# Attention and a routed FFN on one core: another order of the last block's stages, of the softmax sums' way through DRAM and of the first gathers of the second table

## The chip, the core and the metric

The kernel runs on one core of a Trainium2 chip. The metric is the time on the device in microseconds (us), lower is better. A profiled execution gives times of single instructions by the engines: TensorE (PE, matmuls; PEld, its weight loads), VectorE (DVE), ScalarE (ACT), GpSimd (POOL) and SyncE (SP, which here only issues DMAs).

## The reference, cut to what matters

All data is float32: x of 4 batches, 1024 tokens and 256 channels.

```python
x = x + attention(_layernorm(x), w_attn, w_proj)   # causal, 16 heads of 16, ALiBi bias
x = x + ffn(_layernorm(x))
# ffn attends, at each of the 1024 positions, over the 4 batches:
qkv = x @ in_proj_w.T + in_proj_b
scores = einsum('tbhd,sbhd->bhts', q, k) * scale   # t, s: the 4 batches; b: 1024 positions
ctx = softmax(scores) applied to v
h = _layernorm(x + ctx @ out_w.T + out_b, ln1_g, ln1_b)
logits = h @ router_w.T + router_b
assign = max of the two best experts' numbers      # 8 experts, so 1 to 7
out = w2[assign] @ gelu(w1[assign] @ h + b1) + b2  # only the assigned expert counts
result = _layernorm(h + out, ln2_g, ln2_b)
```

A token has exactly one expert, so the kernel computes one expert for a token, in tiles of 128 tokens of the same expert.

## The kernel before, in words

**Attention** is cut into 20 units. Chunks c = 0 to 2 of 256 query columns give four units each (one a batch: u0 to u11, two blocks of 128 queries), chunk 3 gives eight units of one block (u12 to u19). A unit has four groups of heads (G = 4), and each group its rounds: scores by PE (`score`, L884), exp by ACT (L892), the causal zeros by POOL (L902), and two rounds later the weighted values by PE (`weigh`, pv, L925), whose extra column gives the sums of the exps. The order of PE's work is written by hand: a loop over pairs p of rounds, with an "E slot" (steps that are mostly DVE's) at 2p and 2p + 1 and a "D slot" (PE steps) between. Steps are put at numbered slots by `at_E` and `at_D`.

The **sums' way** of a unit: after its last pv, `weigh` writes y to DRAM (SP, L941). `load_sums` reads the sums back, one to a partition (L948); `invert` takes reciprocals on DVE (L955) and writes them, r, to DRAM (L956); `load_y` reads r spread over each head's channels, su (L971), and y, yc (L974); `divide` multiplies them on DVE (L979); `project` does the output projection on PE (op, L991) and adds to x on DVE (L984). With e the first pair behind the unit, these stand at E slots 2e + 3, 2e + 5, 2e + 6, 2e + 9 and at D slot e + 5 (one earlier each, from `invert` on, for u18).

A **front** (`front(i)`, L1421) takes block i of 128 positions with its 4 batches up to the router, as a generator of stages: norm (L725, L731, L747), transposes (utp, L1448), qkvp (L1469), pr and sc (scores over batches on DVE, L1490 and L1491), softmax (tot is its sum), pv (L1510), ctp (L1533), ao (L1556) with its add (L1561), the second norm (rstd_h), key, best, rank, expert and hot (L1576 to L1605: the router's choice as 0 or 1), rows written to DRAM (L1609), place (L1614: a token's rank within its expert, by a matmul with a triangle). Fronts 0 to 6 are queued behind their chunk's last unit and yield ("E" or "D", cost); `take_E` and `take_D` run at most so much cost in a slot (2.5 or 3.6, and 5.6). Front 7 goes last, behind attention.

**Routing** (class `Routing`): `tabulate_first` runs behind six fronts and gives the full tiles among them (18), `tabulate_rest` behind all eight, 20 more. `counts` sums `so_far` over partitions by a matmul with ones (L1106), compares with the multiples of 128 (L1115) and reduces (L1120), which is the tiles of each expert. `own_of` (L1125) marks a column's expert, `looked_up` (L1137, L1140) finds the place of its first tile, in_tile (L1229, L1234, L1237) marks the tile of each token, `spread` makes at_places (L1099, its rank within the tile), and `who` (L1266) multiplies them on PE: the row of each place of a tile. From it come rows_ (gather), out_rows (scatter) and at_w (the expert's weight address).

**Tiles** (class `Experts`): `fetch` issues the gather of a tile by POOL (indirect DMA into one of 18 buffers given, L1647) and its w1 by SP (L1663, 8 buffers); a tile reaches mtp (transpose, L1674) at the third step behind its gather, then hid (L1687), gelu (ACT, L1696), oe (L1703; three PSUM buffers of a pair of tiles). Each pair is finished by stats_v (DVE), rstd_v (POOL pow, L731), o (DVE, L1720 and L1723) and two outs (POOL memset and indirect DMA, L1729 and L1730), spread over the next steps.

**The tail's order**: after attention come the tail's pools, normalise of the last groups, the last unit's sums and w2 (L1997), eight `fetch`es, `project_slots` (L1028: op of u19, with no way through DRAM), and then a loop: in each pair of slots four `tile_step`s between E and D slots. While a front is not done, `tile_step` returns at once when only HELD_BACK = 6 tiles are left or when the tile work costed for PE is ahead of that for DVE. `tabulate_rest` is put at the head of the running stages by front 7's last one. Here is the step of the loop:

```python
def tile_step():
    if queue or running and part.placed < NT:
        if experts.left() <= HELD_BACK or busy["PE"] > busy["DVE"]:
            return
```

Of the kernel before, what the change touches and what calls it, by code (L numbers as in the profile page):

```python
# [37 lines left out]
P = 128  # L38
# [29 lines left out]
HELD_BACK = 6  # L68
TILE_PE, TILE_DVE = 2.6, 1.6
# [503 lines left out]
def fast_layer(ctx: ExitStack, tc: tile.TileContext, odd, x, wq, wk, wv, wp, w_in, w_out, w_r,  # L573
# [146 lines left out]
    def norm_stats(src, n, name, tag=""):  # L720
        stats = small.tile([P, B, 6], F32, tag="stats" + tag, name=f"stats_{name}")
        mv = small.tile([P, B, 2], F32, tag="mv" + tag, name=f"mv_{name}")
        rstd = small.tile([P, B], F32, tag="rstd" + tag, name=f"rstd_{name}")
        for i in range(n):
            nc.vector.bn_stats(stats[:, i], src(i))  # L725
            nc.vector.bn_aggr(mv[:, i], stats[:, i])
        nc.vector.tensor_scalar(rstd[:, :n], mv[:, :n, 1], EPS, None, ALU.add)
        return mv, rstd

# [334 lines left out]
    class Routing:  # L1064
# [6 lines left out]
        def prepare(self):  # L1071
# [4 lines left out]
            self.firsts = numbered("firsts", [P, N_COLUMNS], [[P, N_COLUMNS]])  # L1076
# [7 lines left out]
            )  # L1084

# [18 lines left out]
        def counts(self, n):  # L1104
            pm = bank(f"counts{n}")
            nc.tensor.matmul(pm[:, :E], ones_bf, self.so_far, start=True, stop=True)  # L1106
            count = keep.tile([P, E], F32, tag="count", name=f"count{n}")
            if n == 0:

                nc.vector.tensor_scalar(count, pm[:, :E], float(P - 1), None, ALU.subtract)  # L1110
            else:
                nc.vector.tensor_copy(count, pm[:, :E])
            some = N_COLUMNS if n else len(FIRST) * B
            full = keep.tile([P, E, N_COLUMNS], F32, tag="full", name=f"full{n}")[:, :, :some]
            nc.vector.tensor_tensor(  # L1115
                full, count.unsqueeze(2).to_broadcast([P, E, some]),
                self.firsts[:, :some].unsqueeze(1).to_broadcast([P, E, some]), ALU.is_gt,
            )
            tiles = const(f"tiles{n}", [P, E])
            nc.vector.tensor_reduce(tiles, full, AX.X, ALU.add)  # L1120
            return tiles

        def own_of(self, lo, hi):
            own = keep.tile([P, N_COLUMNS, E], F32, tag="own", name=f"own{lo}")[:, lo:hi]
            nc.vector.tensor_tensor(  # L1125
                own, con(IOTA, E).unsqueeze(1).to_broadcast([P, hi - lo, E]),
                self.expert.rearrange("p k t -> p (k t)")[:, lo:hi].unsqueeze(2).to_broadcast(
                    [P, hi - lo, E]
                ), ALU.is_equal,
            )  # L1130
            return own
# [22 lines left out]
        def tabulate_first(self):  # L1154
# [3 lines left out]
            self.tiles = self.counts(0)  # L1158
# [8 lines left out]
            own = self.own_of(0, n)  # L1167
# [9 lines left out]
            yield from self.tabulate(0, 0, N_FIRST, nowhere, self.past(0, N_TILES, self.until, "whose0"))  # L1177

        def tabulate_rest(self):

            yield "D", 0.3
            lo, hi = len(FIRST) * B, N_COLUMNS
            self.split(lo, hi)
            tiles = self.counts(1)
# [6 lines left out]
            nc.vector.tensor_tensor(before, until, tiles, ALU.subtract)  # L1191
            found = const("found", [P, N_COLUMNS])
            self.looked_up(found, self.own_of(0, N_COLUMNS), before, "behind_of")
            nc.vector.tensor_tensor(found, found, self.by_128, ALU.add)

            mine, tile_of = found[:, :lo], self.tile_of[:, :lo]
            nc.vector.tensor_tensor(mine, mine, tile_of, ALU.subtract)
            nc.vector.tensor_tensor(mine, mine, self.late[:, :lo], ALU.mult)
            nc.vector.tensor_tensor(mine, mine, tile_of, ALU.add)
# [14 lines left out]
        def tabulate(self, n, first, end, tile_of, whose):  # L1214
# [11 lines left out]
            if n == 0:  # L1226
# [7 lines left out]
            nc.vector.tensor_scalar(  # L1234
                in_tile[:, :, 1], in_tile[:, :, 2], row_no, None, ALU.mult
            )
# [4 lines left out]
            who = table("who_f", [P, 3, n_tiles])  # L1241
            if n == 0:
                nc.vector.memset(who, 0.0)
# [17 lines left out]
            else:  # L1261
                at_place = late["at_place"]
                self.spread(at_place[-1], len(FIRST) * B, N_COLUMNS)
# [6 lines left out]
                self.whose = whose()  # L1270
                nc.vector.tensor_copy(who, pm)
# [10 lines left out]
            block, at_t = (table(name, [P, n_tiles], I32) for name in ("block", "at_t"))  # L1282
            nc.vector.tensor_scalar(  # L1283
                who[:, 2], who[:, 2], -float(NOWHERE), float(NOWHERE), ALU.mult, ALU.add
            )
            nc.vector.tensor_tensor(who[:, 1], who[:, 1], who[:, 2], ALU.add)
# [4 lines left out]
                who[:, 1], block, float(P), who[:, 1], ALU.mult, ALU.add  # L1291
            )
            nc.vector.scalar_tensor_tensor(
                out_rows, at_t, float(T), who[:, 1], ALU.mult, ALU.add
# [126 lines left out]
    def front(i, fact, more, last):  # L1421
# [6 lines left out]
        yield "E", 0  # L1428
# [71 lines left out]
        yield "E", 0  # L1500
# [46 lines left out]
        if not last:  # L1547
            if i < PC * (NC - 2):
                yield "E", 0
            yield "D", 2.4  # L1550
            ct = flipped(ctx_, "ct")
        yield "D", 1.8
        for t in range(B):
# [7 lines left out]
            nc.vector.tensor_tensor(u_[:, t], u_[:, t], pm, ALU.add)  # L1561
            if t == 1:
                yield "d", 1.8
        yield "E", 2.6

        taken = small.tile([P, B, E], F32, tag="taken", name=f"taken_{i}", bufs=2)
        nc.vector.tensor_copy(taken, u_[:, :, C:])
        mv, rstd = norm_stats(lambda t: u[:, t], B, f"h_{i}")
        yield "E", 0
# [36 lines left out]
        yield "E", 2.2  # L1606
        nc.vector.tensor_tensor(u, u, wide(row(G1)), ALU.mult)
# [3 lines left out]

        pm = bank(f"place_{i}")
# [12 lines left out]
        nc.vector.tensor_reduce(part.rank[:, i], rank, AX.X, ALU.add)  # L1625
        here = small.tile([P, E], F32, tag="here", name=f"here_{i}")
        nc.vector.tensor_reduce(here, hot.rearrange("p t e -> p e t"), AX.X, ALU.add)
        nc.vector.tensor_tensor(part.so_far, part.so_far, here, ALU.add)
        part.placed += 1
        if part.placed == len(FIRST):  # L1630
            running.insert(0, Running(part.tabulate_first()))
        if part.placed == NT:
            running.insert(0, Running(part.tabulate_rest()))
# [106 lines left out]
    class Experts:  # L1740
# [21 lines left out]
        def left(self):  # L1762
            return (len(tiles_to_do) + len(self.fetched)
                    + len(self.under_way) + len(self.done) + len(self.finishing))

        def advance(self):
# [5 lines left out]
            if len(self.done) == 2 or self.done and not self.under_way:  # L1772
                late["n_oe"] += late["n_oe"] % 2
                self.finishing.append((len(self.done), finish_tiles(self.done)))
                next(self.finishing[-1][1])
                self.done = []
# [16 lines left out]
    class Running:  # L1793
        def __init__(self, stages):
            self.stages, self.slot, self.was = stages, -9, None
            self.next()
# [20 lines left out]
    def take_E(cost=0.0, most=E_SLOT):  # L1817


        slot[0] += 1  # L1820
        start_fronts()
        for it in list(running):
            if it.kind in ("E", "P") and it.slot < slot[0] - (it.kind == "P"):
                if cost and cost + it.cost > most:
                    continue
# [3 lines left out]
                if it.kind == "end":  # L1829
                    running.remove(it)  # L1830
        return cost

    def take_D(cost):

        slot[0] += 1
        for it in list(running):
            while it.kind[0] in "Dd":
                if it.kind == "DQ" and ("qkv",) in held:
                    break
                if it.kind != "d" or it.slot < slot[0]:  # L1840
                    if it.slot >= slot[0] - (it.was == "E"):
                        break
                if cost and cost + it.cost > D_SLOT:
# [24 lines left out]
    for u, (n, i, size) in enumerate(units):  # L1868
# [15 lines left out]
        if u < last_unit:  # L1884
            late_ = u == last_unit - 1
            at_E(2 * e + 3, lambda u=u: load_sums(u))
            at_E(2 * e + 5 - late_, lambda u=u: invert(u))
            at_E(2 * e + 6 - late_, lambda u=u: load_y(u))
            at_E(2 * e + 9 - late_, lambda u=u: divide(u))
            at_D(e + 5 - late_, 0.9 * size, lambda u=u: project(u))  # L1890
        if b == B - 1 and u < last_unit:
            at_E(2 * e + 11, lambda c=c, i=i, size=size: queue.extend(
# [52 lines left out]
    def D_slot(p):  # L1945
# [3 lines left out]
        return take_D(sum(cost for cost, _ in todo))  # L1949
# [21 lines left out]
    for p in range(len(rounds) // 2):  # L1971
# [10 lines left out]
        E_slot(2 * p + 1, most)  # L1982
# [4 lines left out]

    tail = ctx.enter_context(pool("tail", 1))
# [4 lines left out]
    for g in range(2, G):  # L1993
        normalise(g)
    load_sums(last_unit)
# [13 lines left out]
    project_slots()  # L2009
    p = len(rounds) // 2  # L2010
    E_slot(2 * p)
    D_slot(p)
    E_slot(2 * p + 1)
    queue.append(front(NT - 1, fact, 1, True))
# [14 lines left out]
    busy = {"PE": 0.0, "DVE": 0.0}  # L2029

    def tile_step():


        if queue or running and part.placed < NT:
            if experts.left() <= HELD_BACK or busy["PE"] > busy["DVE"]:
                return
            busy["PE"] += TILE_PE
            busy["DVE"] += TILE_DVE
        experts.fetch()
        experts.advance()  # L2040

# [4 lines left out]
    for k in range(len(FIRST) // 2):  # L2046
        at_E(2 * p + 6 + 4 * k, lambda k=k: part.spread(
            late["at_place"][k], 2 * B * k, 2 * B * (k + 1)
        ))
    at_E(2 * p + 24, check_sums)  # L2050
    fetching.clear()
    while queue or running or experts.left() or of_E or of_D:
        p += 1
        start_fronts()
# [101 lines left out]
```

## Time and profile before

| | us |
|---|---|
| median of 3 runs (lowest to highest) | 875.63 (867.71 to 877.36) |
| the profiled execution | 877.08 |
| its span, first to last instruction | 875.3 |
| PE, PEld busy | 767.9 (88%), 576.8 (66%) |
| DVE, ACT, POOL busy | 535.7 (61%), 393.1 (45%), 253.1 (29%) |
| end of the last pv (attention) | 656.70 |
| start of utp, of qkvp in front 7 | 687.17, 696.12 |
| front 7's pv on DVE begins / ao begins on PE | 744.75 / 755.37 |
| front 7's hot is made (DVE) | 768.15 |
| first gather of the second table | 789.89 |
| last out issued / end | 867.18 / 875.3 |

How to read it: times count from the span's first instruction. A row of the timeline has the start, the duration, engine, line, operation, result <- operands by the program's names and, in brackets, the idle time ahead of it and what ended it. In a table of stages each engine has its busy time and, in parentheses, its instructions; PEclk is the granted clock of TensorE as a share of the full one, then the mean share of the 16 DMA engines and GB/s. The mean granted clock of the span is 0.931. A row of waits has what waited, for what, and microseconds in total, times, and the longest.

### The profile page before, as it was taken

How to read it: one execution, taken by the hardware profiler on the slowest of the kernel's cores; microseconds unless marked ns; L12 is line 12 of the kernel's file. 1: busy time of each engine (PE TensorE's matmuls, PEld its weight loads, DVE VectorE, ACT ScalarE, POOL GpSimd, SP SyncE). 2: the span in 40 equal slices, each digit the busy share in tenths (PEclk: the TensorE clock that was granted, in tenths of full speed). 3: DMA queues.
4: the chain of work that ended last, by engine and by line, in shares of the span. 5: the costliest groups of instructions: out<-in, count | busy, mean ns of one | idle time of the engine just before them, and what ended most of it. 6: DMA issues, size and time to landing. Idle time of an engine off the chain costs nothing.

```text
span 875.3 us, 22574 instructions
## 1 busy us (share of the span) xinstructions
PE 767.9 (88%) x8981; PEld 576.8 (66%) x8981; DVE 535.7 (61%) x1275; ACT 393.1 (45%) x548; POOL 253.1 (29%) x359
## 2 busy tenths in 40 slices
PE   3998889998999999999999989989995997654993
PEld 2776667666666676666777767677773785543882
DVE  7334346339467773866687483793797668682454
ACT  1453436556555755655654554565461223100220
POOL 5432114212111211112121211121122448115685
PEclk9897979999999999999999999999996999865997
DMA  6445454524423333332554343244215563017550
GB/s 203 116 106 162 113 155 129 156 74 154 134 76 107 94 100 124 98 110 79 153 146 142 112 138 120 75 117 140 74 40 161 161 191 119 8 43 240 170 156 30
DMA packets 79108, 105.60 MB, mean 121 GB/s; under 512 B 19928, under 2 KB 59155, under 8 KB 78484
## 3 DMA queue, kind: packets, MB, share of 16 engines
q1 hardware_dynamic: 73548, 89.22, 34.7%
q0 software_dynamic: 4864, 14.16, 5.2%
q8 instruction: 73, 1.20, 0.6%
q10 hardware_dynamic: 584, 0.70, 0.3%
q14 instruction: 39, 0.32, 0.1%
HBM read 67.58 MB, written 35.12 MB: 117 GB/s over the span
## 4 chain that ended last, share of the span: by engine, by line
PE 58%; DVE 16%; issue 10%; DMA 6%; POOL 6%; ACT 2%; SPq 2%; POOLq 0%; DVEq 0%; ACTq 0%
PE sk L884 16%; PE pv L925 10%; PE qkvp L1469 8%; PE qkp L803 5%; PE op L991 3%; PE vp L824 3%; PE ao L1556 2%; DVE pv L1510 2%; POOL given L1647 2%; PE hid L1687 2%; POOL out_dram L1730 2%; PE oe L1703 2%; ACT p L892 2%; DVE pv L1543 1%; DMA yc<-y 1%
## 5 line engine op out<-in xcount | busy, mean ns | idle before, releaser
L892 ACT ACTIVATE p<-sk 128x1024 f32<-128x1024 f32 (+1 forms) x320 | 289.7, 937 | 210.2 <-PE sk L884 197.9
L902 POOL TENSOR_SCALAR_AFFINE_SELECT p<-p 128x512 f32<-128x512 f32 (+1 forms) x160 | 105.6, 663 | 453.2 <-ACT p L892 450.9
L884 PE MATMUL sk<-slots 32*128 32x128 f32 (+1 forms) x3456 | 217.8, 336 | 21.1 <-ACT p L892 16.2
L884 PEld LDWEIGHTS sk<-slots 32*128 32x128 f32 x3456 | 162.3, 191 | 77.7 <-ACT p L892 31.6
L925 PE MATMUL pv<-p,v 128*32 128x128 f32 (+1 forms) x3456 | 146.5, 318 | 0.0
L925 PEld LDWEIGHTS pv<-p,v 128*32 128x32 f32 x3456 | 98.2, 113 | 36.8 <-issue 7.8
L1469 PE MATMUL qkvp<-w_in,ut 128*128 128x512 f32 (+1 forms) x256 | 92.4, 495 | 0.2 <-DVE x L984 0.2
L803 PE MATMUL qkp<-xt,wqk 128*128 128x256 f32 x256 | 66.7, 406 | 0.7 <-ACT xt L793 0.7
L1469 PEld LDWEIGHTS qkvp<-w_in,ut 128*128 128x128 f32 x256 | 44.4, 190 | 31.1 <-issue 25.7
L803 PEld LDWEIGHTS qkp<-xt,wqk 128*128 128x128 f32 x256 | 50.2, 202 | 11.6 <-issue 2.0
L1687 PE MATMUL hid<-mt,w 128*128 128x128 f32 x304 | 49.9, 304 | 6.0 <-DMA w<-in_w_dram 3.0
L1476 DVE COPY qkv<-qkvp 128x264 f32<-128x264 f32 x28 | 12.1, 432 | 68.6 <-PE qkvp L1469 68.6
L1687 PEld LDWEIGHTS hid<-mt,w 128*128 128x128 f32 x304 | 44.2, 208 | 12.8 <-ACT mt L1676 5.6
L1647 POOL DMA_INDIRECT given<-rows,rows x38 | 42.2, 1109 | 33.2 <-DVE who_f L1283 14.4
L1696 ACT ACTIVATE ge<-hid 128x256 f32<-128x256 f32 x38 | 14.6, 383 | 82.6 <-PE hid L1691 44.2
L808 DVE COPY kq<-qkp 128x512 f32<-128x512 f32 x32 | 21.9, 686 | 46.6 <-PE qkp L803 46.3
L1478 ACT COPY qkv<-qkvp 128x512 f32<-128x512 f32 (+1 forms) x36 | 20.2, 562 | 48.5 <-PE qkvp L1469 45.2
L1510 DVE TENSOR_TENSOR pv<-qkv,sc 128x1024 f32<-128x1024 f32 x32 | 39.6, 1241 | 3.9 <-PE ctp L1533 3.7
L1703 PE MATMUL oe<-w,ge 128*128 x152 | 41.8, 400 | 0.1
L1730 POOL DMA_INDIRECT out_dram<-o,out_rows x38 | 39.4, 1037 | 6.9 <-issue 6.9
L1490 DVE TENSOR_TENSOR pr<-qkv 128x1024 f32<-128x1024 f32 x32 | 39.9, 1246 | 0.0
L991 PE MATMUL op<-wp,yc 128*128 128x256 f32 x124 | 34.6, 421 | 5.9 <-DVE yc L979 5.8
(259 smaller groups left out, 1003.9 us busy)
## 6 DMA issues: line engine op xcount, KB each, us to landing
slots<-k SPq DMA_DIRECT2D x128, 80.0 KB
w<-in_w_dram SPq DMA_DIRECT2D x38, 256.0 KB
k<-kq SPq DMA_DIRECT2D x32, 256.0 KB
y<-yt SPq DMA_DIRECT2D x24, 256.0 KB
v<-v SPq DMA_DIRECT2D x20, 288.0 KB
v<-v SPq DMA_DIRECT2D x4, 1152.0 KB
x<-in_x_dram SPq DMA_DIRECT2D x16, 256.0 KB
rows<-x SPq DMA_DIRECT2D x32, 128.0 KB
```

Of the source, the lines that this page charges most:

```text
L803: nc.tensor.matmul(pm[:, k * W:(k + 1) * W], wqk[:, k, cc, half * P:(half + 1) * P], xt[:, cc], start=cc == 0, stop=cc == CC - 1,)
L884: nc.tensor.matmul(ps[h // 2][:, h % 2, width:to], kt[rows_, kb * P:(kb + 1) * P], qt[rows_, off:], start=True, stop=True,)
L892: nc.scalar.activation(pt[:, :, :width], ps[pair][:, :, :width], AF.Exp, scale=1.0 / math.sqrt(D))
L902: nc.gpsimd.affine_select(blocks, blocks, pattern=[[0, 2], [0, size], [1, P]], compare_op=ALU.is_ge, fill=0.0, base=0, channel_multiplier=-1,)
L925: nc.tensor.matmul(pv[h * S:(h + 1) * S, off:], vt[:, kb, at:at + S], pts[h // 2][:, h % 2, at_p:to], start=r == 0 and k == 0, stop=own an ...
L991: nc.tensor.matmul(pm[:, i * C:(i + 1) * C], yc[:, cc, i * P:(i + 1) * P], wp_sb[:, cc], start=cc == 0, stop=cc == CC - 1,)
L1469: nc.tensor.matmul(pq, ut[:, cc, t * P:(t + 1) * P], w_in_sb[:, cc, lo:hi], start=cc == 0, stop=cc == CC - 1,)
L1510: nc.vector.tensor_tensor(pr.rearrange("p s (h d) -> p s h d", d=D), qkv[:, :, 2 * C:3 * C].rearrange("p s (h d) -> p s h d", d=D), sc[:, ...
L1647: nc.gpsimd.indirect_dma_start(out=self.hx, out_offset=None, in_=t.rows_of, in_offset=bass.IndirectOffsetOnAxis(ap=t.rows_[:, self.j:self. ...
L1687: nc.tensor.matmul(ph[:, fc], self.w1[:, cc, fc * P:(fc + 1) * P], mt[:, cc], start=cc == 0, stop=False,)
L1703: nc.tensor.matmul(self.v, ge[:, fc], late["w2"][:, bass.ds(at + fc * C, C)], start=fc == 0, stop=False,)
L1730: ins = nc.gpsimd.indirect_dma_start(out=out.rearrange("t n c -> (t n) c"), out_offset=bass.IndirectOffsetOnAxis(ap=t.table.out_rows[:, t. ...
```

## The change

1. The sums' steps of u4 to u18 go to E slots 2e + 1, 2e + 3, 2e + 4, 2e + 6, and project to D slot e + 3. u0 to u3 stay, and u18 no longer has slots of its own. A chunk's front is queued at 2e + 7 in place of 2e + 11.
2. Stages get a kind "N" (no cost, a new slot all the same). Front 7 is "alone": `take_E` runs several of its E stages in a row, and D stages of it needn't wait a slot. Its second norm is taken position by position right behind each ao (`norm_one`), and the copy `taken` comes behind the stats.
3. In the tail, normalise, load_sums and project_slots stand ahead of the pools; front 7 is put at the head of the running stages. Tiles are taken by a credit: each slot adds the cost it took and STEP = 1.0, at most 8.0; a tile costs 2.6; HELD_BACK is 4, of tiles whose stages have not begun; none is taken from "near" on (once hot of front 7 is made).
4. Counts: front 7's hot is added to the count by five matmuls into one bank (`count_all`), so no here and so_far of block 7; the tiles of an expert are (count + 127) >> 7. `own` of the first 24 columns, their by and tile_of (`prepare_rest(0)`) and block 6's own, split and spread (`prepare_rest(1)`) are done ahead. The row_no product of the second in_tile goes to ACT.
5. After the loop two `tile_step(False)` (no finish of tiles), then `tabulate_rest` in a row, then six `fetch`es and normal steps; check_sums at the eighth.

```diff
-            late_ = u == last_unit - 1
-            at_E(2 * e + 3, lambda u=u: load_sums(u))
-            at_E(2 * e + 5 - late_, lambda u=u: invert(u))
-            at_E(2 * e + 6 - late_, lambda u=u: load_y(u))
-            at_E(2 * e + 9 - late_, lambda u=u: divide(u))
-            at_D(e + 5 - late_, 0.9 * size, lambda u=u: project(u))
+            for k, what in enumerate((load_sums, invert, load_y, divide)):
+                at = ((3, 5, 6, 9) if c == 0 else (1, 3, 4, 6))[k]
+                at_E(2 * e + at, lambda u=u, what=what: what(u))
+            at_D(e + (5 if c == 0 else 3), 0.9 * size, lambda u=u: project(u))
...
+            if last:
+                norm_one(stats, t, u[:, t])
...
+        if last:
+            held["near"] = True
...
+        if last:
+            part.count_all(hot)
...
+        def count_all(self, hot):
+            self.all = bank("counts_all")[:, :E]
+            for k, of_one in enumerate([self.so_far] + [hot[:, t] for t in range(B)]):
+                nc.tensor.matmul(self.all, ones_bf, of_one, start=k == 0, stop=k == B)
...
         def tabulate_rest(self):
+            lo, hi = N_COLUMNS - B, N_COLUMNS
+            whole = keep.tile([P, E], I32, tag="count", name="whole_all")
+            nc.vector.tensor_scalar(whole, self.all, float(P - 1), None, ALU.add)
+            nc.vector.tensor_single_scalar(whole, whole, 7, op=ALU.logical_shift_right)
...
+                nc.scalar.activation(
+                    in_tile[:, :, 1], in_tile[:, :, 2], AF.Identity, scale=row_no
+                )
...
-                self.spread(at_place[-1], len(FIRST) * B, N_COLUMNS)
+                self.spread(at_place[-1][:, B:], N_COLUMNS - B, N_COLUMNS)
...
+    for g in range(2, G):
+        normalise(g)
+    load_sums(last_unit)
+    project_slots()
     tail = ctx.enter_context(pool("tail", 1))
...
+    while queue or running:
+        for take in (lambda: E_slot(k, 99.0), lambda: 0.0 * D_slot(p, 99.0)):
+            credit = min(credit + take() + STEP, MOST_CREDIT)
+            while credit >= TILE_PE and experts.waiting() > HELD_BACK and "near" not in held:
+                tile_step()
+                credit -= TILE_PE
+        if part.placed == NT - 1 and not prepared:
+            prepared = True
+            part.prepare_rest(1)
+        k, p = k + 1, p + 1
+    for _ in range(HELD_BACK // 2):
+        tile_step(False)
+    for _ in part.tabulate_rest():
+        pass
+    for _ in range(6):
+        experts.fetch()
+    n = 0
+    while experts.left():
         tile_step()
+        n += 1
+        if n == 8:
+            check_sums()
```

## The prediction

> **What bounds the kernel now.** I read the table of stages first (busy time of each engine in chosen stretches), then TensorE's idle times, then the waits of the sums' way, then POOL's rows.
>
> ```profile
> core 0: us, PE busy (x) PEld busy (x) DVE busy (x) ACT busy (x) POOL busy (x), PEclk, DMA share, GB/s
> 441.00:656.70 215.70, 201.86 (x3636) 158.95 (x3630) 148.20 (x327) 118.97 (x147) 41.75 (x63) 0.96 0.39 110
> 656.70:696.10 39.40, 28.95 (x154) 23.09 (x155) 27.62 (x80) 8.89 (x20) 11.81 (x11) 0.78 0.48 150
> 696.10:743.10 47.00, 42.03 (x252) 32.91 (x250) 35.12 (x80) 14.28 (x33) 29.51 (x36) 1.00 0.53 166
> 743.10:768.40 25.30, 13.51 (x84) 12.45 (x85) 16.53 (x44) 3.56 (x8) 4.00 (x7) 0.78 0.05 16
> 768.40:789.90 21.50, 11.61 (x81) 9.93 (x80) 18.27 (x58) 1.14 (x3) 3.81 (x7) 0.66 0.11 37
> 789.90:860.50 70.60, 60.81 (x381) 52.56 (x381) 30.75 (x91) 13.59 (x40) 50.28 (x68) 0.87 0.57 180
> ```
>
> Up to 656.70 (the last pv; times from it are written +x) TensorE is the bound: 201.86 of 215.70 us. From 743 to 790 nothing is: PE works 25 of 47 us, because front 7 (block 7 on its way to the router) and the second table form one chain. Its waits are these:
>
> ```profile
> 746.04 9.50 PE L1533 MATMUL ctp<-ident,pv 128*128 128x128 f32 x64 [5.85 <-DVE pv L1510]
> 768.40 0.18 PE L1614 MATMUL place<-hot,lower 128*128 128x32 bf16 x1 [8.85 <-DVE hot L1605]
> 786.51 1.76 PE L1266 MATMUL who<-in_tile,at_places 128*128 128x60 bf16 x32 [8.18 <-DVE in_tile L1237]
> 793.44 0.66 PE L1674 MATMUL mtp<-ident,given 128*128 128x128 f32 x2 [5.18 <-DMA given<-rows,rows]
> ```
>
> The brackets hold 28.1 us of PE idle time. After 789.90 the 20 tiles of the second table bind PE (60.81 of 70.60) with POOL close behind (50.28).
>
> The page's list of waits shows the sums' way, and SP's rows one unit of it (u15, a unit of one block):
>
> ```profile
> DVE yc L979 <- DMA yc<-y: 11.3, 6, 4.5
> PEld op L991 <- DVE yc L979: 8.6, 7, 2.7
> ```
>
> ```profile
> 558.05 0.37 SPq L956 DMA_DIRECT2D r<-inverse  x1
> 560.67 0.59 SPq L971 DMA_DIRECT2D su<-r  x1
> 562.58 0.58 SPq L974 DMA_DIRECT2D yc<-y  x1
> ```
>
> So already now 6 of 19 divides waited, 11.3 us in all. On POOL the first gather of the rest, the last pow and the last out:
>
> ```profile
> 789.89 1.09 POOL L1647 DMA_INDIRECT given<-rows,rows  x1 [9.34 <-DVE at_t L1288]
> 862.15 0.72 POOL L731 TENSOR_TENSOR rstd_v<-rstd_v,minus_half 128x2 f32<-128x2 f32 x1 [0.49 <-DVE rstd_v L727]
> 867.18 0.98 POOL L1730 DMA_INDIRECT out_dram<-o,out_rows  x1 [0.19 <-issue]
> ```
>
> From the last out's end (868.16) to the span's end are 7.1 us.
>
> **The change, part by part.** The sum is made against the profiled execution: 877.08 us, span 875.3, so 1.8 us around the span. It lies 1.45 us above the median of 875.63; I subtract that at the end.
>
> *1. Sums sooner (units 4 to 18, 15 units).* The route's four steps stand at slots 1, 3, 4, 6 behind a unit in place of 3, 5, 6, 9; project moves to the D slot right behind divide. Between invert and op lie now three E slots, before four and a D slot. Price of the chain from rows: invert to r 3.2 (554.84 to 558.05), r to the first su 2.6, su to the last yc 1.9, landing of the last yc 2.1 (564.7; the larger c=2 unit of 290 us took 5.5, 296.63 to 302.1), divide 0.4. Sum 10.2 for one-block units, 13.6 for two-block ones. TensorE's work in the same slots, counted by matmul groups, is 8.5 to 14 us. Where it is less, DVE waits in divide (queued behind it: the fronts' pr/sc and the copies out of PSUM), then PE at op. Slot by slot that happens in u4, u6, u8, u11, u14, u17 and u18, 1 to 3 us each; some waits of today (1.32 us of PE at 441) are in it. Bounds: 0, and every unit at the middle of the gap, (13.6 - 11.3) x 15 = 34.5. I take 4.4, near the low end, since the row of before (4 slots) shows waits of 8.6 us on PE's loads, but only 1.3 us of PE idle. SP too: sums<-y is issued right behind the y write, so SP's queue stands some 2 us longer at it, and slots<-k loads queue there; they are a unit ahead, cost nothing while that lead holds, and if not, a slots wait of up to 1 us a unit (bound 15, in the range). Work that moves ahead of the last pv: ctp of block 6 (1.95), op of u18 (1.1), who of tiles of table 0 (0.6): 3.6 us, which leave the tail. **Term: +8.**
>
> *2. Tail's start.* normalise and project_slots go ahead of the pools; x is complete near +5 (before +9.8). w2 is still issued on SP then, w1 behind it, and 9 gathers run on POOL's queue. In PE's new order three tiles' hid stand ahead of utp_7. Alone w2 (1.835 MB) took 6.1 us, 300 GB/s; w1 and gathers together 280 to 290 GB/s (674.6 to 682). With both queues sharing that, I put w1 of the first tile at +18 and utp_7 at +30, as today (+30.5): no gain, because the transfer hides the sooner x add. Bounds: utp_7 at +22 (w1 lands as if alone) and +36.
>
> The packets above share 16 engines. [...]
>
> *3. Front 7 in a row.* qkvp ends at +50 (before +56.0), the four pairs of pr/sc (2.47 each) at +60.7, and 10.6 us of tile work, rank of block 6 and spreads stand on DVE ahead of tot: +73.6 (before +86.4). pv, ctp, ao take what they took: ao to rstd_h 93.5, hot 99.3 (before +111.6), rank +102.1. Norm of block 7 per t behind ao hides three of four stats pairs (0.6 each). Gain so far 12.3.
>
> *4. Table.* Between rank (771.07) and at_t (789.7) DVE did: o and stats of held tiles 8.3 (771.29 to 779.65), counts compare and reduce 0.9, own 0.42, late product chain 0.6, row_no product 0.4, spread 1.2. Of these the tile work is stopped once "near" is set; the counts become three small operations (0.5); own of 24 columns, the late chain and 28 of 32 places are done ahead, on DVE beside PE work; the row_no product goes to ACT (ACT has 1.14 of 21.5 us; bounds 0.4 and 1.0). Rank to in_tile is then 5.4 instead of 13.7. in_tile +107.5, who to +109.8, first gather +111.3, before +133.2. **Terms 2 to 4: -21.9**, bounds -30 and -14.
>
> *5. Rest.* Before: 789.89 to the end, 85.4 us. POOL did 20 gathers x 1.32, 24 outs x 1.30, 10 pow x 1.0 = 67.6 in 78.3 us. In the new order 7 gathers go first and, since fewer tiles were finished, 10 outs and 4 pow of the first table come behind them: 26.4 + 39 + 14 = 79.4, with 3 us of gaps and the 7.1 of the drain 89.5. pow stands behind gathers, o waits for pow, and oe (3 pairs of PSUM) for o: PE waits on POOL. By PE alone: 4 held tiles, then 20 x 2.69 (823.16 to 825.85) and 14.9 of drain, 84.2. I take POOL. **Term: +4.1**, bounds -1.2 and +8. Held tiles meet a slow clock (0.66 in that row; steps of about 4 us, 5 us in all if nothing warms it).
>
> The row of 768 to 790 grants 0.66 with three idle stretches in it. [...]
>
> *6. Counting matmuls* (5 of 8 columns, 0.2 us), I32 shift, check_sums at the eighth step: on engines with idle time, 0; if check_sums (4 small DVE operations) met a late o, 1.
>
> Sum: 877.1 + 8 - 21.9 + 4.1 = 867.3; against the median 865.8. **866.**
>
> **Rivals.**
> - *A, the tail pays fully.* DVE hides the sums' waits (term 1: 3.6) and POOL keeps up (-1.2): 877.1 + 3.6 - 21.9 - 1.2 - 1.45 = 856; with utp_7 at +22, 848. For it: PE idled only 13.8 us in the whole of 441 to 656.7. Against: the POOL count, and DMA at the tail's start.
> - *B, eaten up.* The stalls take 14 us (0.95 in each of 15 units): term 1 is 18, 876. For it: 6 divides wait today with more room. The change would then move the wait out of the tail into attention.
> - *C, slower.* One mechanism: op in PE's order waits for the DRAM route in every unit, 2.3 us x 15 = 34.5, term 1 is 38: 896. It decides against the change from 0.95 us a unit, and beyond 1% from 1.5 us. For it: two-block yc landings of 5.5 us. Against: seven of the 15 units are one-block (2.1 us).
> - *No effect of 1:* that the sums were never late; then term 1 is 3.6 and A's attention half holds.
>
> **How the numbers follow.** Forecast .45 (860 to 871), A .25 (848 to 859), B .17 (871 to 884), C .13 (885 to 896). A measurement of this kernel tells about 1% from no change, 866.9 to 884.4 being the same. Faster: A and .27 of the forecast, .52; same: .18 and most of B, .34; slower: C and a rest of B, .14. The range leaves C and the lowest .07 of A out: 850 to 884.
>
> **What would show it.** Step 1: PE idle ahead of op, and the last pv near 665; past 675 is B or C, below 661 A. Steps 2 to 4: utp_7 at 30 us behind the last pv, hot at 99, first gather of the rest at 111. Step 5: POOL busy over .85 from there on, and PE waiting for o or pow; PE busy over .9 there is A. I am wrong if the gathers' first row is later than 125 us behind the last pv, or if attention is shorter than before.

## The result, and the profile after

The changed kernel takes 923.53 us (median of 4 runs, 922.91 to 924.75), the kernel before 876.24 us in the same comparison: ratio 1.0564, 95% interval 1.0496 to 1.0632. It is slower by 47 us, where 866 was forecast. The profiled execution has a span of 921.2 us and a mean granted clock of 0.919.

The table of stages of the changed kernel, cut where the work is cut: chunk 3 up to the last pv, then to qkvp of front 7, to its tot, to counts_all, to the first gather of the rest, to the last 14 us:

```profile
core 0: us, PE busy (x) PEld busy (x) DVE busy (x) ACT busy (x) POOL busy (x), PEclk, DMA share, GB/s
445.00:722.10 277.10, 248.51 (x4319) 195.45 (x4311) 183.29 (x391) 142.27 (x177) 46.88 (x77) 0.92 0.37 104
722.10:760.00 37.90, 26.82 (x154) 22.30 (x151) 21.60 (x64) 9.07 (x21) 17.43 (x17) 0.82 0.70 241
760.00:791.80 31.80, 27.89 (x157) 20.80 (x155) 21.53 (x49) 10.72 (x23) 11.75 (x15) 1.00 0.39 124
791.80:817.70 25.90, 15.78 (x106) 14.54 (x107) 19.31 (x54) 4.21 (x10) 8.32 (x11) 0.84 0.06 21
817.70:828.30 10.60, 10.60 (x91) 9.30 (x90) 9.82 (x35) 2.18 (x6) 0.03 (x1) 0.75 0.15 51
828.30:907.00 78.70, 67.31 (x432) 58.35 (x431) 45.16 (x132) 14.89 (x45) 59.99 (x85) 0.93 0.56 172
907.00:921.20 14.20, 0.00 (x0) 0.00 (x0) 2.72 (x10) 0.00 (x0) 5.86 (x10) 0.66 0.07 19
```

Read the boundaries first. The last pv is at 722.2 in place of 656.7: attention is 65.5 us longer. From there to the end are 199.1 in place of 218.6: the tail is 19.5 us shorter. The difference of the spans, 45.9, is the sum of these two. Within the tail the second table is no longer a hole: from 817.7 to 828.3 PE is busy throughout.

The list of waits says what holds attention up (what waited, for what, us in total, times, longest):

```profile
PEld op L1003 <- DVE yc L991: 49.5, 15, 8.0
...
PE op L1003 <- DVE yc L991: 45.0, 15, 7.6
...
DVE yc L991 <- DMA yc<-y: 32.4, 10, 7.2
```

PE's idle time ahead of op is 45.0 us, where attention of before had 5.0 (5.8 with u18's op, which stood behind the last pv there). One unit, u8, shows its making. SP's rows (the sums' way is 302.84 sums, 309.52 r, 311.87 and 313.89 su, 312.52 and 314.51 yc):

```profile
300.66 0.36 SPq L953 DMA_DIRECT2D y<-yt  x1
302.84 0.56 SPq L960 DMA_DIRECT2D sums<-y  x1
303.49 0.83 SPq L852 DMA_DIRECT2D v<-v  x1
304.66 0.36 SPq L828 DMA_DIRECT2D k<-kq  x1
305.12 1.90 SPq L867 DMA_DIRECT2D slots<-k  x4
307.07 2.29 SPq L1489 DMA_DIRECT2D rows<-x  x4
309.52 0.32 SPq L968 DMA_DIRECT2D r<-inverse  x1
311.87 0.60 SPq L983 DMA_DIRECT2D su<-r  x1
312.52 1.31 SPq L986 DMA_DIRECT2D yc<-y  x1
313.89 0.58 SPq L983 DMA_DIRECT2D su<-r  x1
314.51 0.58 SPq L986 DMA_DIRECT2D yc<-y  x1
```

DVE's rows of the same unit, invert and divide:

```profile
305.89 0.34 DVE L967 RECIPROCAL inverse<-sums 128x32 f32<-128x32 f32 x1
...
319.79 0.69 DVE L991 TENSOR_TENSOR yc<-yc,su 128x512 f32<-128x512 f32 x1 [5.29 <-DMA slots<-k]
```

And PE's, over the same time:

```profile
305.93 1.56 PE L896 MATMUL sk<-slots 32*128 32x256 f32 x16
...
310.21 1.72 PE L937 MATMUL pv<-p,v 128*32 128x256 f32 x32
311.86 1.30 PE L896 MATMUL sk<-slots 32*128 32x256 f32 x16
320.54 3.78 PE L1003 MATMUL op<-wp,yc 128*128 128x256 f32 x8 [7.38 <-DVE yc L991]
```

From the y write (300.66) to op (320.54) the way takes 19.9 us: SP stands 2.2 us until y is in DRAM, the sums land and DVE inverts them at 305.9, r leaves behind other transfers at 309.5, su can be read 2.3 us later, the last read is issued at 314.5 and landed by 319.8. (The bracket of divide names `slots`, whose loads SP issued behind that read; when yc itself landed the trace doesn't say.) PE passes invert's slot with the sk at 305.93, just as invert runs, and is out of work 7.2 us later, at 313.2. And op itself then takes 3.78 us at a granted clock of 0.50; in u5, with no wait ahead of it, the same eight matmuls take 1.99 at 1.00. The durations of all op matmuls (ns, least, median, largest), before and after:

```profile
L991 PE MATMUL op<-wp,yc x124: 379/379/796, 83.4 to 668.3; 128*128 128x256 f32 x124
```

```profile
L1003 PE MATMUL op<-wp,yc x124: 379/618/796, 82.9 to 715.9; 128*128 128x256 f32 x124
```

So this wait is paid twice: 7.38 us as idle time and 1.79 us (3.78 for 1.99) as a lowered clock in the op behind it. By PE's own rows in attention, idle time ahead of op went from 5.0 to 45.0 (+40.0), op's own time from 31.6 to 45.9 (+14.3: the slow ops of ten units are 13.0 of it, and 1.1 is u18's op, moved in), ao and pv gained 5.5, other idle time 3.8, the rest 1.9: 65.5.

The marks of the tail, in us behind the last pv:

| | before | forecast | after |
|---|---|---|---|
| first hid (waits for w1) | 19.5 | 18 | 18.0 |
| utp of front 7 | 30.5 | 30 | 28.9 |
| qkvp ends | 56.0 | 50 | 48.9 |
| tot | 86.4 | 73.6 | 69.6 |
| hot | 111.5 | 99.3 | 95.3 |
| first gather of the rest | 133.2 | 111.3 | 106.1 |
| from there to the end | 85.4 | 89.5 | 92.9 |

### The profile page after: what moved, and what is told of

It is laid out like the page before. It is cut to its first block, busy times and chain, and to the rows that moved or that the text cites. A ratio compares the mean times of both kernels' runs of the same rounds, so it can differ in the third digit from the quotient of the medians.

```text
span 921.2 us, 22578 instructions
## 1 busy us (share of the span) xinstructions
PE 780.8 (85%) x8985; PEld 586.7 (64%) x8985; DVE 535.0 (58%) x1281; ACT 393.2 (43%) x549; POOL 248.9 (27%) x359
## 5 line engine op out<-in xcount | busy, mean ns | idle before, releaser
L937 PE MATMUL pv<-p,v 128*32 128x128 f32 (+1 forms) x3456 | 148.8, 322 | 0.0
L937 PEld LDWEIGHTS pv<-p,v 128*32 128x32 f32 x3456 | 100.5, 115 | 36.6 <-issue 7.1
L1519 PE MATMUL qkvp<-w_in,ut 128*128 128x512 f32 (+1 forms) x256 | 92.9, 497 | 0.0
L1003 PE MATMUL op<-wp,yc 128*128 128x256 f32 x124 | 46.2, 530 | 45.0 <-DVE yc L991 45.0
L1003 PEld LDWEIGHTS op<-wp,yc 128*128 128x128 f32 x124 | 30.3, 260 | 55.6 <-DVE yc L991 49.5
L1758 ACT ACTIVATE ge<-hid 128x256 f32<-128x256 f32 x38 | 14.6, 383 | 101.6 <-PE hid L1753 70.5
L815 PEld LDWEIGHTS qkp<-xt,wqk 128*128 128x128 f32 x256 | 49.1, 199 | 11.9 <-issue 2.3
L1765 PE MATMUL oe<-w,ge 128*128 x152 | 43.2, 410 | 14.1 <-DVE o L1782 9.2
L1749 PEld LDWEIGHTS hid<-mt,w 128*128 128x128 f32 x304 | 43.8, 208 | 16.5 <-issue 11.2
L1526 DVE COPY qkv<-qkvp 128x264 f32<-128x264 f32 x28 | 12.1, 431 | 66.2 <-PE qkvp L1519 66.2
L1709 POOL DMA_INDIRECT given<-rows,rows x38 | 40.4, 1064 | 25.6 <-PE hid L1753 15.4
L991 DVE TENSOR_TENSOR yc<-yc,su 128x512 f32<-128x512 f32 (+1 forms) x19 | 11.3, 593 | 50.1 <-DMA yc<-y 32.4
```

The costliest lines, as they stand in the source:

```text
L815: nc.tensor.matmul(pm[:, k * W:(k + 1) * W], wqk[:, k, cc, half * P:(half + 1) * P], xt[:, cc], start=cc == 0, stop=cc == CC - 1,)
L937: nc.tensor.matmul(pv[h * S:(h + 1) * S, off:], vt[:, kb, at:at + S], pts[h // 2][:, h % 2, at_p:to], start=r == 0 and k == 0, stop=own an ...
L1003: nc.tensor.matmul(pm[:, i * C:(i + 1) * C], yc[:, cc, i * P:(i + 1) * P], wp_sb[:, cc], start=cc == 0, stop=cc == CC - 1,)
L1519: nc.tensor.matmul(pq, ut[:, cc, t * P:(t + 1) * P], w_in_sb[:, cc, lo:hi], start=cc == 0, stop=cc == CC - 1,)
L1709: nc.gpsimd.indirect_dma_start(out=self.hx, out_offset=None, in_=t.rows_of, in_offset=bass.IndirectOffsetOnAxis(ap=t.rows_[:, self.j:self. ...
L1749: nc.tensor.matmul(ph[:, fc], self.w1[:, cc, fc * P:(fc + 1) * P], mt[:, cc], start=cc == 0, stop=False,)
```

## The experiments

Theory W: PE, whose order is fixed, comes to op before the sums' way is done. Rival F: the new kinds of stages and take_E's loop disorder the fronts. All kernels beside the kernel before on the same chip; its medians in the three groups (e1 to e4, e5 to e8, e9 to e12) were 876.66, 874.69 and 878.48. "Idle at op" is PE's idle time ahead of op behind divide; "last pv" and "tail" (from the last pv to the end) come from the profiled execution. The three groups ran on three chips, so kernels of different groups are best compared through the kernel before. Up to u3's op all kernels but e8 carry out the same instructions in the same order, and yet this op begins between 137.9 and 143.4 us: so far apart are single executions without any edit.

| kernel | median us | ratio to before (95%) | idle at op | last pv | tail |
|---|---|---|---|---|---|
| before | 876.24 | | 5.8 | 656.7 | 218.6 |
| after | 923.53 | 1.0564 (1.0496 to 1.0632) | 45.0 | 722.2 | 199.1 |
| e1 after, old sums | 882.13 | 1.0068 (1.0027 to 1.0108) | 4.1 | 667.5 | 215.0 |
| e2 before, sooner sums | 929.94 | 1.0620 (1.0549 to 1.0690) | 54.0 | 722.6 | 207.1 |
| e3 after, op a pair later | 890.97 | 1.0172 (1.0113 to 1.0232) | 15.9 | 677.9 | 215.1 |
| e4 after, read soon, used late | 884.90 | 1.0126 (1.0074 to 1.0178) | 9.3 | 663.9 | 216.4 |
| e5 after, sooner for u15, u18 only | 871.49 | 0.9977 (0.9945 to 1.0010) | 14.8 | 674.8 | 195.2 |
| e6 e5, one stage to a slot | 861.13 | 0.9846 (0.9798 to 0.9895) | 8.8 | 666.9 | 191.8 |
| e7 e5, gathers between outs | 870.08 | 0.9971 (0.9930 to 1.0012) | 17.0 | 676.6 | 192.7 |
| e8 after, yc read with the sums | 912.80 | unclear (902 to 919) | 40.7 | 711.6 | 196.0 |
| e9 before, sooner for u15 only | 873.42 | 0.9948 (0.9920 to 0.9975) | 6.6 | 651.7 | 217.9 |
| e10 e1, one stage to a slot | 863.74 | 0.9824 (0.9783 to 0.9865) | 12.8 | 667.7 | 195.3 |
| e11 e6, u18 later | 852.90 | 0.9713 (0.9672 to 0.9754) | 6.4 | 654.2 | 196.7 |
| e12 e11, two w1 ahead of w2 | 857.22 | 0.9761 (0.9719 to 0.9804) | 6.4 | 655.8 | 200.4 |

**e1, the sums at the old slots.**

```diff
-                at = ((3, 5, 6, 9) if c == 0 else (1, 3, 4, 6))[k]
-            at_D(e + (5 if c == 0 else 3), 0.9 * size, lambda u=u: project(u))
+            at, op = ((1, 3, 4, 6), 3) if u == last_unit - 1 else ((3, 5, 6, 9), 5)
+            at_D(e + op, 0.9 * size, lambda u=u: project(u))
...
-            at_E(2 * e + (11 if c == 0 else 7), lambda c=c, i=i, size=size: queue.extend(
+            at_E(2 * e + 11, lambda c=c, i=i, size=size: queue.extend(
```

> The changed kernel with the sums' steps of u4 to u17 at the old slots (3, 5, 6, 9 and e + 5) and the fronts queued at 2e + 11; only u18 keeps the new ones. Theory W (TensorE waits at op for the sums' way, and op runs at a lowered clock behind each wait): PE idle ahead of op falls from 45 to about 5 us, the last pv from 722 to about 660, and with the tail of the changed kernel (199 us) the time is 861 (855 to 868). Theory F (the new kinds of stages and take_E's loop disorder the fronts within attention): the last pv stays above 700 and the time above 900.

The idle time at op fell to 4.1 us and the time by 41 us, as W has it; F would have left it above 900. But 882 is not 861: attention ended at 667.5, and the tail, which W took over at 199, was 215. So the new tail owed its length to something in the sums' part.

**e2, the sooner sums alone, in the kernel before** (the slots and queueing of the change, nothing else).

> The kernel before with the sums' steps, project and the fronts' queueing of the changed kernel, nothing else. Theory W: PE idle ahead of op about 45 us, the last pv at about 718, the time 935 (925 to 945). Theory F: the last pv within 10 us of 657, the time 876 to 886.

929.94, with 54 us of idle time at op: the whole loss is there without any other part of the change. W stands, F falls as the cause of this loss. (Project and the queueing of the fronts move along here; no run moves the queueing of all fronts alone.) The line of waits:

```profile
PE op L991 <- DVE yc L979: 54.0, 16, 7.7
```

**e3, op one pair later** (slots 1, 3, 4, 8 and e + 4).

> The changed kernel with the reads as soon as there (1, 3, 4), but divide at 8 and project at e + 4, one pair of rounds later (u18 as there). Theory W: a pair holds 4 to 6 us of TensorE's work, as long as most of the waits (3.0 on average, 7.6 the longest), so that 5 to 12 us of idle time are left at op, the last pv is at 668 to 678 and the time 869 to 880. Theory S (SP's queue, stopped at the sooner reads, holds back the loads of slots): above 900, with PE waiting at sk for slots.

Idle time 15.9 us in 9 waits, the longest 3.3: one pair takes two thirds of it, two pairs (e1) nearly all. That is more than W's 5 to 12 us, but 4.3 of it stand in u1 and u2, whose slots no kernel changes. The time missed W's range by 11 us, mostly since the tail is 215, as in e1, and not 199; it lies 9 us above e1. S, above 900, falls.

**e4, read soon, use late** (slots 1, 3, 4, 9 and e + 5).

> The changed kernel with the reads as soon as there (1, 3, 4), but divide and project at the old places (9 and e + 5) and the fronts queued at 2e + 11 (u18 as in the change). Theory W: at most 3 us of idle time at op, time as with all the steps at the old slots, within 4 us (857 to 865). Theory S: more than 10 us above that, with PE waiting at sk for slots.

Like e1 (the intervals overlap, attention 3.6 us shorter): sooner reads cost nothing and bring nothing. Of the 9.3 us of idle time, three times what W allowed, 5.5 stand in u1 and u2, which the edit leaves alone. S falls; PE's waits for slots were 7.4 us (10.4 in the changed kernel).

**e5, sooner for u15 and u18 only, others at the old slots.**

```diff
+            soon = u == last_unit - 1 or c == NC - 1 and b == B - 1
+            at, op = ((1, 3, 4, 6), 3) if soon else ((3, 5, 6, 9), 5)
...
+            at_E(2 * e + (7 if soon else 11), lambda c=c, i=i, size=size: queue.extend(
```

> The changed kernel with the sooner sums for two units only: u15, on which front 6 waits (its queueing 2e + 7 stays too), and u18; all the others at the old slots. Theory W2 (the sooner sums pay only where a front starts behind them: front 6 done sooner shortens the tail by 11 to 16 us; in all other units they buy nothing and cost their wait): attention as with the old slots plus one wait (667 + 3 us), the tail as in the changed kernel (199 to 202), time 870 (864 to 876). Rival R (the short tail of the changed kernel comes from its own steps, or from fronts that got on during the waits): tail 212 to 216 as with the old slots, time 882.

871.49, as W2 said, with a tail of 195.2, 19.8 us less than e1's. The time fits by some luck: attention ended 5 us later than W2 had it, and the tail is 4 us shorter. Why a sooner front 6 is worth so much here, e9 and e10 tell. R falls: without the long waits the tail is no longer than in the changed kernel.

**e6, one E stage to a slot in chunk 3 and the tail.** take_E gives several E stages in a row to every front where the slot's limit is above 2.5, that is in chunk 3 and the tail, not only to front 7:

```diff
-                if it.kind != "E" or not (it.alone or most > E_SLOT):
+                if it.kind != "E" or not it.alone:
```

> The kernel of e5 with take_E giving only one E stage of a front to a slot in chunk 3, as before the change (several only for front 7). Theory F2 (several stages in a slot put DVE ahead of what PE waits for in chunk 3, where the kernel with the old slots lost 6.8 us to the one before): chunk 3 shorter by 4 to 7 us, but fronts later; time 3 to 6 us below e5. Rival: the same within 2 us, the loss being the moved work of ctp, op and who (3.6 us).

10.4 us below e5, more than expected, and 1.5% faster than before. By the profiles 7.9 us of it are in attention and 3.4 in the tail.

**e7, gathers between outs** (e5 without the six fetches behind the table).

> The kernel of e5 without the six fetches behind the second table, so that gathers stand between outs as before the change. If the gathers in a row make POOL the bound of the rest (theory of the prediction's step 5, +4.1): 2 to 5 us faster than e5, with less PE idle time at oe. If they buy sooner tiles (PE waited 12 us at mtp before the change): 2 to 8 us slower, with PE idle at mtp.

Neither: the two medians lie 1.4 us apart and their intervals overlap. The stretch from the first gather is 88.7 us in place of 90.8, PE's wait at oe 11.9 in place of 13.0. The order of the gathers decides little.

**e8, yc read with the sums.**

```diff
         )
+        if u == last_unit:
+            return
...
+            nc.sync.dma_start(yc[:, cc], heads_of(u)[at, :D])
```

> The changed kernel with the reads of yc right behind the read of the sums (they don't need r), so that behind invert only r and the reads of su are left. Theory W: the last link of the wait (issue 1.9 us, and part of the landing of 2 to 5 us) is gone in 15 units: PE idle at op falls from 45 to 15 to 25 us, and op's own time by a third of that; time 880 to 900. Rival (the wait is set by the front end, y to the sums to invert, which runs late because DVE is behind): idle stays above 38 us, time above 912.

Idle time fell by 4 us only, as the rival had it (its four runs lie between 902 and 919), so the reads of yc are not the link that binds. The rival's reason, an invert that runs late, is not shown: invert starts only 0.6 us on average behind PE's passing of its slot. With the way cut into links for u4 to u18 (means in us, from the issues and starts in the rows; the last line's reads are su alone):

| | y to sums | sums to invert | invert to r | r to last read | to divide | to op | whole |
|---|---|---|---|---|---|---|---|
| before | 8.5 | 6.0 | 2.8 | 5.0 | 7.8 | 1.7 | 31.8 |
| after | 2.9 | 4.9 | 1.5 | 5.6 | 3.8 | 0.8 | 19.4 |
| e2 | 2.8 | 4.5 | 1.6 | 5.8 | 4.2 | 0.7 | 19.5 |
| e8 | 2.8 | 5.0 | 2.1 | 5.3 | 3.3 | 0.7 | 19.1 |

Three kernels with these slots give the same 19 us on average: two trips through DRAM, one behind the other, with SP and DVE between. It is no floor: in the changed kernel single units take 14.4 (u18) to 22.5 us (u15), and other transfers on SP stand between the links. Before, the way had 31.8 us, 12 more than it took here.

**e9, sooner for u15 only, in the kernel before.**

> The kernel before with the sooner sums and the sooner queueing of front 6 for u15 alone. Theory W2 (a sooner front 6 is worth some 11 us of the tail by itself, as the tail of 207 us with all the sums sooner showed against 218.6): one wait more in attention (+3 us), tail 207 to 210, time 866 to 869. Rival R (the tail got shorter because 15 waits gave the fronts time): time 876 to 880.

The tail is 217.9: W2 falls as it was put. A sooner front 6 alone buys nothing in the tail of before, and the 11.5 us by which e2's tail is shorter are not its doing. In e2 utp of front 7 is at +23.0 where before and e9 have +30.5 and +30.3, and e2 differs from e9 in op of u18 (ahead of the last pv) and in its longer attention; which of the two it is was not tried. What goes with it: in e2 the first table is done 8.6 us sooner (its last who ends at +4.0, for +12.6).

**e10, e1 with one E stage to a slot.**

> The kernel of e1 (old slots but for u18) with one E stage to a slot in chunk 3. With e1, e5 and e6 this makes four: old or sooner u15, several stages or one. Theory F2: the two effects add up, so 882 less the 10.4 us between e5 and e6: 872 (868 to 876). Rival (one stage to a slot pays only where front 6 starts sooner): 880 to 884.

863.74, 18 us below e1 (20 when each is set against the kernel before on its own chip), in neither range and below even the 872 of adding up: one stage to a slot is worth 18 to 20 us with the old slots, 10 with a sooner u15. All of it is in the tail. First, front 7 starts sooner there. In e1 four tiles stand ahead of its utp in PE's order, and the first of them waits 9.7 us for w1; in e10 none does, since the first table is done at +4.0 (its last who ends) in place of -12.9. PE's rows, e1 and then e10:

```profile
682.53 1.19 PE L1749 MATMUL hid<-mt,w 128*128 128x128 f32 x4 [9.73 <-DMA w<-in_w_dram]
...
696.97 1.04 PE L1498 MATMUL utp<-ident,u 128*128 128x128 f32 x8
```

```profile
681.86 2.81 PE L1498 MATMUL utp<-ident,u 128*128 128x128 f32 x8 [0.15 <-ACT u L755]
```

Second, DVE's order. Its rows in the tail of e1:

```profile
739.49 0.19 DVE L1639 TENSOR_REDUCE best<-key 128x4 f32<-128x32 f32 x1
...
743.10 0.19 DVE L1663 TENSOR_TENSOR hot<-low_con,expert 128x32 bf16<-128x32 f32 x1
743.21 1.22 DVE L1667 TENSOR_TENSOR u<-u,rows 128x1024 f32<-128x1024 f32 x1
744.47 1.23 DVE L1668 TENSOR_TENSOR u<-u,rows 128x1024 f32<-128x1024 f32 x1
...
748.78 0.57 DVE L1554 TENSOR_REDUCE tot<-sc 128x64 f32<-128x256 f32 x1
```

and in that of e10:

```profile
728.16 0.58 DVE L1554 TENSOR_REDUCE tot<-sc 128x64 f32<-128x256 f32 x1
...
732.12 0.17 DVE L1639 TENSOR_REDUCE best<-key 128x4 f32<-128x32 f32 x1
...
742.12 0.19 DVE L1663 TENSOR_TENSOR hot<-low_con,expert 128x32 bf16<-128x32 f32 x1
```

best and hot are front 6's, tot is front 7's, and front 7 is what the end waits for. In e1 the whole rank of front 6 stands in a row ahead of tot; in e10 it comes in pieces behind it. Tot is at +60.4 in place of +81.3; 15.4 of these 20.9 us are utp's (+14.1 in place of +29.5), the other 5.5 lie between utp and tot. In the changed kernel this did not show, because u15's sooner sums had let front 6 start sooner: its hot came at +32.6 (+31.4 in e5, without the long waits), against +75.7 in e1. e5's utp comes at +27.2, 2.3 us ahead of e1's, its tot at +68.0, 13.3 ahead: there the rank's place counts most. So a sooner front 6 is worth 20 us of tail with several stages in a row (e1 to e5), 3.5 with one (e10 to e6), nothing in the order of before (e9).

**e11, u18 as before the change, front 7 one slot pair later.**

```diff
+            if u == last_unit - 1:
+                at, op = (3, 4, 5, 8), 4
...
+    E_slot(2 * p, 99.0)
+    D_slot(p, 99.0)
     running.insert(0, Running(front(NT - 1, fact, 1, True), True))
```

> The kernel of e6 with u18's sums and op as before the change (3, 4, 5, 8 and e + 4, so behind the last pv), and front 7 put in one slot pair later. Theory W: the last unit loses its 7 us of wait and slow op (attention is 3 us late at the last but one unit of e6, 10 at its end): last pv at 659 to 662, front 7 waits for w1's tiles anyway (TensorE stood 9 us at the first hid in the changed kernel), time 854 to 858. Rival (front 7's chain starts later by as much as attention ends sooner): 860 to 863.

852.90: faster than both kernels, ratio 0.9713 (0.9672 to 0.9754). Attention ends at 654.2, where e6 had 666.9; the tail gave back 4.9 of the 12.7. How much of the gain over e6 is the edit's is not shown: 6.5 of the 12.7 us lie ahead of u17's op, up to which the two kernels do the same, and e12, with the order of e11, took 857.22. W's range (854 to 858) lies between these two times.

**e12, the first two tiles' w1 ahead of w2.**

> The kernel of e11 with the first two tiles' w1 issued ahead of w2. If the 9 us that TensorE stood at the first hid are the path of front 7 (its utp stands behind three tiles in TensorE's order; the prediction's step 2, bound +22 in place of +30): first hid 8 to 10 us behind the last pv, time 4 to 8 us below e11. Rival (w2 comes later and oe waits for it, or DVE's other work sets tot): within 2 us of e11.

4.3 us above e11, but the edit did not do what it was to do. SP's rows behind the last pv, e11 and then e12:

```profile
657.07 1.53 SPq L2073 DMA_DIRECT2D w<-in_w_dram  x3
670.93 2.90 SPq L1725 DMA_DIRECT2D w<-in_w_dram  x4
```

```profile
658.64 1.54 SPq L2084 DMA_DIRECT2D w<-in_w_dram  x3
672.51 2.90 SPq L1725 DMA_DIRECT2D w<-in_w_dram  x4
```

The first row of each is w2 (the profile leaves the numbers out), the second the first w1. W2 goes first in both: in this order the first table is done at +12.9 only, so that the eight `fetch`es find no tile. The rows of every engine have the same order in the two kernels. So e12 decides between neither theory, and its 4.3 us show how far two kernels of one order can lie apart (why, stays open). Whether the 9 us at the first hid of the changed kernel are a reserve it doesn't test; e10 shows utp of front 7 some 15 us sooner where no tile that waits for w1 stands ahead of it.

## Why the prediction was wrong, point by point

- **Step 1 (+8) failed; attention took 65.5.** The step that failed is the price of the waits, 4.4 us, and under it "TensorE's work in the same slots ... is 8.5 to 14 us", whose middle, 11.3, was set against the chain from invert on. The chain was near: 10.2 and 13.6 us were estimated, and invert to op measured 9.2 to 14.6 (on average 11.2 in one-block and 12.1 in two-block units). So was its start: PE passes invert's slot (with the first sk behind it) 7.0 us behind the y write on average, and invert starts at 7.7. But PE's work from that slot to op was 9.4 us on average, 7.2 to 13.5 and under 10.5 in 13 of the 15 units (9.3 on average in e2, too). So 12.37 us from the slot to op stand against 9.43 of work, 2.94 in each unit and 44.1 in all; counted from the y write it is 19.4 against 16.5. 13 of the 15 units waited, 0.4 to 7.6 us; I had named seven and missed u7, u9, u10, u12, u15 and u16, among them the longest wait of all.
- **The low price leaned on a misread row.** "Only 1.3 us of PE idle" is one wait of before; its profile has five, and there PE's work from invert's slot to op was 17.0 us:

```profile
PE op L991 <- DVE yc L979: 5.8, 5, 2.3
```

- **A term was missing from it:** behind its longer waits op ran slow. A two-block op took 3.78 us in place of 1.99 behind waits of 2.85 us or more (3.38 in u4); over ten units the slow ops cost 13.0 us. The sum has no term for it, though step 5 prices a slow clock for the held tiles. Rival C (2.3 us a unit, 896) had the mechanism and the sign; by this missing term, and with 2.9 us a unit, its price was too low, and its chance of .13 far too low. The row of waits that spoke for it (6 divides late already, with three slots more) was shown and set aside.
- **Step 2 held:** w1 at +18.0 as estimated from the shared rate (from 722 to 740 the gathers' queue moved 2.48 MB and SP's 2.57, 282 GB/s in all), utp at +28.9 for +30.
- **Steps 3 and 4 (-21.9): -27.1** to the first gather. The size was near, the reason only in part: in the changed kernel front 6 was out of the way when front 7 came, thanks to u15's sooner sums and its own sooner queueing. Without these (e1) the first gather is at +121.6, 11.6 us ahead of before, and the several stages in a row, which I had costed at nothing, cost 18 us there (e10).
- **Step 5 (+4.1): +7.5** in the changed kernel. PE waited 10.2 us for oe in three pieces, two of them on o, POOL was busy in 60.0 of 78.7 us, or in 70 (.89) with the gaps under 0.35 us between its instructions, which the prediction's prices hold; so POOL may well bind here. e7 shows that the gathers in a row are not the cause. In this stretch 22 tiles now run in place of 20, and 30 outs in place of 24; what else the 7.5 us hold was not taken apart.
- **Step 6 held:** the counts and check_sums appear in no wait beyond counts_all's own (7.2 us for hot, 8.9 before).
- The tail as a whole came out at -19.5 for -17.8, with some luck: steps 2 to 4 gave 5.2 us more than forecast, step 5 cost 3.4 more. The sum was lost in term 1.

## What to carry to other kernels

When a step is moved sooner in a hand-written order, take from a trace, unit by unit, the whole way from the first thing it needs (here the y write) to its use, and the work of the waiting engine over the same stretch; here it was 19.4 us against 16.5, and a middle of estimates hid the difference. A wait on an engine that is the bound costs its length and, here behind every wait of 3.0 us and more, a slower clock after it (up to 3.78 us in place of 1.99 for a two-block op). A rule that lets work of one kind run in a row is to be read for everything it lets run, not only for the item that it was made for. And a run decides between theories only if its trace shows that the edit changed the order that it was meant to change.

## What the runs showed of the hardware

- Waits of PE at op ahead of the last pv, in all 14 profiles: behind 58 waits of up to 1.32 us op ran at full speed (1.99 us for eight matmuls, 1.13 for four). Behind all 24 of 3.0 us and more it was slow, at least in part (up to 3.78 and 2.08 us). Of 37 from 1.39 to 2.86 us 25 were followed by a slow op: 2.04 us in u17 of the changed kernel was, 2.86 us in u7 of e8 was not. Behind u8's wait of 7.38 us the granted clock was 0.50 through the whole op; waits of 2.85, 3.09 and 2.04 us were enough for 0.50, in u7, u16 and u17 of the changed kernel, and 1.86 us in u9 left it at 1.00.
- Reading y back right behind its write held SP for 1.8 to 2.2 us between the two issues where no other transfer stood between (u7 to u10 and u18).
